# More token columns fetched by SyncE and ScalarE: 102 and 83 in place of 96 and 52

## The chip, the core and the metric

The kernel runs on one core of a Trainium2 chip. The core has five engines that each work through a stream of their own, in order: TensorE (PE, matrix products; PEld is its loading of weights), VectorE (DVE), ScalarE (ACT), GpSimd (POOL) and SyncE (SP, which only issues transfers and waits). They meet through semaphores. ACTq, POOLq and SPq are the issuing side of an engine; ACTq issues transfers and starts ScalarE's activations. Time is device microseconds of one execution; smaller is better.

## What is computed

A recommendation model for 16384 samples: 32 token indices a sample into a table of 50000 x 300 floats, three fields of 20 indices and four of one into small tables of 64 columns, means and concatenation to 748 features, three dense layers with relu, and a sigmoid.

```python
tok = word_emb[token_idx].mean(axis=1)
e1 = emb_mh1[mh1_idx].mean(axis=1)
...
emb = jnp.concatenate([tok, e1, e2, e3, o1, o2, o3, o4], axis=1)
wide = (wide_mh1[mh1_idx].sum(axis=(1, 2)) + ...)[:, None]
h = jax.nn.relu(emb @ W1 + b1)
h = jax.nn.relu(h @ W2 + b2)
h = jax.nn.relu(h @ W3 + b3)
return jax.nn.sigmoid(h @ Wd + bd + wide)
```

## The kernel before

**Tiles and steps.** The samples go in 128 tiles of 128, one sample on each partition. The small tables are not gathered: for each tile the kernel builds one-hot matrices and multiplies them into counts, and the counts times the tables give the sums of the embeddings. That takes 11 steps a tile (STEPS), so the program is a loop of 128 x 11 + 27 = 1435 steps (line 1118). All of it is unrolled: the loop writes the streams of all five engines in one fixed order, and each engine keeps to that order.

**A step.** DVE makes the one-hots of the next step (`hot`, line 776), ScalarE scales half of them in place (line 783), PE multiplies the present step's one-hots into `pc` (line 795), and ScalarE moves the result to `cnt` (line 797). Between these, PE takes a share of the previous tile's table sums (`pg`, line 829) and of the dense layers (`ph`, line 952), whose results ScalarE evicts to `odd` and `even` (line 963).

**Token rows.** A tile has 32 columns of token indices, two to a group, 16 groups. Normally GpSimd fetches a column by one indirect DMA of 128 rows (`gather`, line 258, issued at line 260) into one of six buffers `tok_rows`, and DVE adds the two columns of a group to a sum in PSUM (`own`, `add_up`, line 588), three groups behind the gather in program order (TOK_LAG). A group falls due every 1 / 1.42 steps (`tokens_by`, line 1067).

**Columns that other queues fetch.** Some columns are left out of POOL's list and fetched row by row by SP (column 31 of a tile, buffers `fetched`) or by ScalarE's queue (column 30, buffers `fetched_scalar`), two buffers each. For such a column:

- 4 steps ahead (COLUMN_AHEAD) `load_column` (line 630) issues a DMA on the fetching queue that brings the 128 indices into one row of `columns`;
- 1 step ahead (COLUMN_LAG) `column_offsets` (line 642) has DVE turn them into byte offsets, two operations on `columns`;
- then `fetch` (line 650) loads the offsets into registers, 32 at a time on SP (LOADS) and 16 on ScalarE (SCALAR_LOADS), by the instruction of line 275, and issues one DMA of 1200 bytes for each of the 128 rows (line 244).

`RowFetches` (line 668) sets which tiles have such a column: from a first step on, one column every FETCH_STEPS steps on SP, and every 128 / SCALAR_RATE steps on ScalarE, each given to the next tile whose sum falls due at least three steps after its rows are issued (FETCH_MARGIN). SP's rows are spread evenly over the steps (`Paced_rows`, line 714). ScalarE's are written into a step in two parts: SCALAR_BEFORE rows in front of the scaling of the one-hots, SCALAR_AFTER behind it (lines 1137 to 1142). SP also issues the loads of the index tiles `it` and `ix` (one pair for two tiles) and the stores of the results.

**Program order.** `Program.record` (line 161) works out which earlier instruction of another engine each one must wait for. A wait holds up everything behind it on that engine.

Of the kernel before, what the change touches and what calls it, by code (L numbers as in the profile page):

```python
# [22 lines left out]
N_TOK, TOK_D = 32, 300  # L23
# [5 lines left out]
TOK_BUFS = 6  # L29
HOT_BUFS = 2  # L30
FETCH_FROM = 4
FETCH_STEPS = 14.5
FETCH_MARGIN = 3.0
FETCH_BUFS = 2
COLUMN_AHEAD = 4
# [1 line left out]
LOADS = 32  # L37
LANES = 8
ROW_SEMAPHORES = 8
SCALAR_FROM = 8  # L40
SCALAR_BEFORE, SCALAR_AFTER = 3, 2
SCALAR_RATE = SCALAR_BEFORE + SCALAR_AFTER
SCALAR_MARGIN = 5.0
SCALAR_LOADS = 16
# [332 lines left out]
def kernel(  # L377
# [679 lines left out]
    tiles = B // P  # L1057
# [13 lines left out]
    def summed_at(t):  # L1071

        n = n_groups * (t + 1) + TOK_LAG
        return n / FRONT_PACE if n < front else FRONT_STEPS + (n - front) / pace
# [2 lines left out]

        return summed_at(t) - 1.0

    by_sync = RowFetches(N_TOK - 1, False, summed_at(FETCH_FROM) - FETCH_STEPS - FETCH_MARGIN, FETCH_STEPS, tiles, LOADS)  # L1080
    scalar_steps = P / SCALAR_RATE
    by_scalar = RowFetches(
        N_TOK - 2, True, int(summed_at(SCALAR_FROM) - scalar_steps - SCALAR_MARGIN), scalar_steps, tiles - 2, SCALAR_LOADS
    )
    sync_rows = Paced_rows(by_sync, FETCH_STEPS)

# [162 lines left out]
```

## Time and profile before

| what | us |
|---|---|
| median of 3 runs | 4987.18 |
| lowest and highest | 4986.96, 4992.43 |
| the profiled execution | 4988.4 |
| its span, first to last instruction | 4986.6 |

| engine | busy us | share of the span |
|---|---|---|
| PE | 4794.8 | 96% |
| POOL | 3739.3 | 75% |
| DVE | 3642.8 | 73% |
| ACT | 2728.2 | 55% |

Issuing a DMA, loading a register and waiting on a semaphore don't count as busy, so SP has no row, and ScalarE's busy time leaves out its rows. Lines that a helper records all carry line 113; they are told apart by the tiles that they write and read (`own<-own,tok_rows` is a token sum). In a row of the timeline stand the start, the time from the first to the end of the last of a merged group, engine, line, operation, tiles and count, and in brackets the idle time ahead of it with what ended it. In a row of waits stand who waited for whom, the total, how often, and the longest.

### The profile page before, as it was taken

To read this page: it belongs to the slowest core of one execution; us is meant where nothing else is said; L and a number is where in the kernel's file an instruction comes from. 1 tells how busy PE (TensorE), PEld (TensorE's weight loads), DVE (VectorE), ACT (ScalarE), POOL (GpSimd) and SP (SyncE) were. 2 spreads that over 40 slices of the span, in tenths; PEclk is the share of its full clock that TensorE was granted. 3 is DMA by queue.
4 is the path that set the end of the run, shared out by engine and by line. 5 is a ranking of instruction groups with operands and counts; after the bars stand their busy time and mean duration, and the time that the engine had idled before them with its cause. 6 is when DMAs were issued, how large, how long until landed. Compare 5 with 4: busy or idle time off the path is not lost.

```text
span 4986.6 us, 110478 instructions
## 1 busy us (share of the span) xinstructions
PE 4794.8 (96%) x36356; PEld 3712.3 (74%) x36356; DVE 3642.8 (73%) x6908; ACT 2728.2 (55%) x3658; POOL 3739.3 (75%) x3955
## 2 busy tenths in 40 slices
PE   6699999999999999999999999999999999999999
PEld 4577777777777777777777777767767888888898
DVE  5777777777777777777777777777777777777763
ACT  5455555555555555555555555555555555555552
POOL 7777777777777777777777777777777777777765
PEclk9899999999999999999999999999999999999999
DMA  7444444444444444444444444444444444444443
GB/s 204 127 130 130 130 131 129 131 130 130 131 131 131 130 130 130 131 131 130 130 131 130 131 131 130 130 131 129 131 130 130 130 131 130 131 131 130 131 120 95
DMA packets 305354, 653.28 MB, mean 131 GB/s; under 512 B 157083, under 2 KB 176667, under 8 KB 304775
## 3 DMA queue, kind: packets, MB, share of 16 engines
q0 software_dynamic: 189504, 606.67, 44.7%
q1 hardware_dynamic: 94471, 31.50, 2.9%
q10 hardware_dynamic: 20800, 8.04, 0.8%
q8 instruction: 284, 4.65, 0.4%
q14 instruction: 295, 2.42, 0.2%
HBM read 645.67 MB, written 0.07 MB: 129 GB/s over the span
## 4 chain that ended last, share of the span: by engine, by line
PE 46%; POOL 16%; DMA 15%; DVE 12%; issue 8%; ACT 1%; ACTq 1%; SPq 1%; DVEq 0%; POOLq 0%
PE ph L113 24%; PE pg L113 16%; POOL tok_rows L260 16%; DMA tok_rows<-in_word_emb_dram,it 15%; PE pc L113 6%; DVE own L113 5%; DVE hot L113 4%; DVE g L113 1%; ACTq L244 1%; SPq L244 1%; ACTq L275 0%; ACT cnt L113 0%; DVE x L113 0%; DVE columns L113 0%; ACT hot L113 0%
## 5 line engine op out<-in xcount | busy, mean ns | idle before, releaser
L260 POOL DMA_INDIRECT tok_rows<-in_word_emb_dram,it x3948 | 3738.4, 947 | 1215.6 <-issue 931.5
L113 DVE TENSOR_TENSOR own<-own,tok_rows 128x300 f32<-128x300 f32 x3601 | 1714.5, 476 | 822.0 <-DMA tok_rows<-in_word_emb_dram,it 746.8
L113 ACT ACTIVATE hot<-hot 64x768 bf16<-64x768 bf16 (+1 forms) x1408 | 1155.3, 821 | 1698.2 <-DVE hot L113 1514.8
L113 PE MATMUL pg<-terms,cnt 128*128 128x195 bf16 x17664 | 1721.6, 249 | 31.0 <-DVE g L113 30.7
L113 PEld LDWEIGHTS pg<-terms,cnt 128*128 128x128 fp8e3 x17664 | 1523.8, 98 | 83.7 <-DVE g L113 39.1
L113 PE MATMUL ph<-x,w_sb 128*128 128x384 f32 (+5 forms) x4932 | 1472.1, 436 | 16.5 <-ACT odd L113 11.3
L113 DVE TENSOR_TENSOR hot<-own,sc 128x1656 bf16<-128x1656 bf16 (+1 forms) x1408 | 1386.6, 985 | 86.0 <-PE pc L113 80.4
L113 ACT ACTIVATE cnt<-pc 128x828 uint16<-128x828 f32 (+1 forms) x1408 | 1186.3, 843 | 257.0 <-PE pc L113 170.8
L113 PEld LDWEIGHTS ph<-x,w_sb 128*128 128x128 f32 (+1 forms) x4932 | 829.8, 191 | 306.5 <-ACT odd L113 20.9
L113 PE MATMUL ph<-odd,w_sb 128*128 128x384 f32 (+2 forms) x3328 | 983.2, 434 | 7.7 <-ACT odd L113 7.3
L113 PEld LDWEIGHTS pc<-hot 128*128 128x128 bf16 x8192 | 589.5, 98 | 494.8 <-issue 217.6
L113 PE MATMUL pc<-hot 128*128 128x138 bf16 x8192 | 733.2, 225 | 92.0 <-ACT hot L113 58.7
L113 PEld LDWEIGHTS ph<-odd,w_sb 128*128 128x128 f32 x3328 | 558.7, 191 | 204.7 <-ACT odd L113 15.8
L113 DVE TENSOR_REDUCE g<-pg 128x130 f32<-128x390 f32 (+1 forms) x512 | 259.7, 507 | 216.0 <-PE pg L113 213.1
L113 ACT ACTIVATE odd<-ph,b_sb 128x384 f32<-128x384 f32 (+2 forms) x515 | 270.0, 524 | 134.4 <-PE ph L113 68.8
L113 PE MATMUL ph<-even,w_sb 128*128 128x384 f32 (+2 forms) x832 | 250.0, 436 | 3.3 <-ACT even L113 2.9
L113 PEld LDWEIGHTS ph<-even,w_sb 128*128 128x128 f32 x832 | 142.3, 191 | 56.8 <-ACT even L113 4.1
L113 DVE TENSOR_TENSOR x<-pc,scale 128x768 f32<-128x768 f32 x127 | 120.9, 952 | 74.8 <-PE pc L113 74.0
L113 ACT ACTIVATE even<-ph,b_sb 128x384 f32<-128x384 f32 (+2 forms) x208 | 108.7, 523 | 88.4 <-PE ph L113 65.8
L113 PE MATMUL pc<-ident,g 128*128 128x128 f32 x762 | 106.5, 276 | 11.7 <-ACT cnt L113 7.5
L113 PEld LDWEIGHTS pc<-ident,g 128*128 128x128 f32 x762 | 82.9, 142 | 15.8 <-ACT cnt L113 11.7
L113 DVE COPY sc<-pc 128x512 bf16<-128x512 bf16 x64 | 44.0, 687 | 55.1 <-PE pc L113 55.0
(54 smaller groups left out, 673.0 us busy)
## 6 DMA issues: line engine op xcount, KB each, us to landing
fetched<-in_word_emb_dram SPq DMA_DIRECT2D x12288, 1.2 KB
fetched_scalar<-in_word_emb_dram ACTq DMA_DIRECT2D x6656, 1.2 KB
tok_rows<-in_word_emb_dram,it POOLq DMA_INDIRECT x3948
ix<-in_idx_dram SPq DMA_DIRECT2D x64, 64.0 KB
w_sb<-in_W_dram SPq DMA_DIRECT2D x6, 512.0 KB
it<-in_idx_dram SPq DMA_DIRECT2D x64, 32.0 KB
w_sb<-in_W_dram SPq DMA_DIRECT2D x1, 2048.0 KB
odd<-in_mh_dram SPq DMA_DIRECT2D x3, 682.5 KB
```

The lines of the kernel that those rows point to most:

```text
L113: lambda: call(*args, **operands), self.name, self.name, aps + list(named.values()), outs
L244: return queue.add_instruction(mybir.InstDMACopy(name=self.nc.get_next_instruction_name(), engine=queue.engine, mode="Copy", ins=whole(sou ...
L260: return self.nc.gpsimd.indirect_dma_start(out=out, out_offset=None, in_=table, in_offset=bass.IndirectOffsetOnAxis(ap=index, axis=0),)
```

## The change

Three constants of the two fetch schedules, and the last tile that SP may fetch for.

```diff
-FETCH_STEPS = 14.5
+FETCH_STEPS = 13.5
...
-SCALAR_BEFORE, SCALAR_AFTER = 3, 2
+SCALAR_BEFORE, SCALAR_AFTER = 5, 3
 SCALAR_RATE = SCALAR_BEFORE + SCALAR_AFTER
...
-    by_sync = RowFetches(N_TOK - 1, False, summed_at(FETCH_FROM) - FETCH_STEPS - FETCH_MARGIN, FETCH_STEPS, tiles, LOADS)
+    by_sync = RowFetches(N_TOK - 1, False, summed_at(FETCH_FROM) - FETCH_STEPS - FETCH_MARGIN, FETCH_STEPS, tiles - 1, LOADS)
```

SP gets 13.5 steps for a column in place of 14.5 and fetches 102 columns in place of 96, the first from step 32.16 in place of 31.16, and none of the last tile. ScalarE issues eight rows a step in place of five, five of them in front of the scaling and three behind; a column takes it 16 steps in place of 25.6, and it fetches 83 columns in place of 52, the first from step 72 in place of 63. GpSimd gathers what is left of 4096 columns: 3911 in place of 3948. No other instruction is added or taken away, but the column loads, offsets and register loads that go with the fetched columns.

## The prediction

> **What bounds the kernel now.** The page comes first: its span, its busy shares and the two groups that handle token rows.
>
> ```profile
> span 4986.6 us, 110478 instructions
> ...
> PE 4794.8 (96%) x36356; PEld 3712.3 (74%) x36356; DVE 3642.8 (73%) x6908; ACT 2728.2 (55%) x3658; POOL 3739.3 (75%) x3955
> ...
> PE 46%; POOL 16%; DMA 15%; DVE 12%; issue 8%; ACT 1%; ACTq 1%; SPq 1%; DVEq 0%; POOLq 0%
> ...
> L260 POOL DMA_INDIRECT tok_rows<-in_word_emb_dram,it x3948 | 3738.4, 947 | 1215.6 <-issue 931.5
> ```
>
> PE is busy 96% and GpSimd (POOL) 75%, so PE looks like the bound. The gather row corrects that. A gather has 947 ns of work and 1215.6 / 3948 = 308 ns of idle ahead of it, 1.255 us together, and 3948 x 1.255 = 4954 us: nearly the whole span. So the next question is whether POOL ever waits. POOL's waits and a piece of the middle timeline answer it.
>
> ```profile
> POOL tok_rows L260 <- issue: 931.5, 3054, 0.3
> POOL tok_rows L260 <- DVE own L113: 166.0, 510, 3.3
> POOL tok_rows L260 <- DVE hot L113: 83.9, 275, 0.3
> ```
>
> ```profile
> 2502.87 0.95 POOL L260 DMA_INDIRECT tok_rows<-in_word_emb_dram,it  x1 [0.30 <-issue]
> ...
> 2504.12 0.95 POOL L260 DMA_INDIRECT tok_rows<-in_word_emb_dram,it  x1 [0.30 <-issue]
> ```
>
> The idle ahead of a gather is 0.3 us whether nothing is waited for (931.5 / 3054) or a DVE signal happens to fall into it (166.0 / 510 = 0.33, 83.9 / 275 = 0.31). POOL runs back to back from end to end. DVE stands behind it:
>
> ```profile
> DVE own L113 <- DMA tok_rows<-in_word_emb_dram,it: 769.8, 757, 4.3
> ...
> DVE own L113 <- DMA fetched<-in_word_emb_dram: 11.2, 3, 6.7
> ```
>
> DVE waits 769.8 us for gathered rows, and only 11.2 us for rows that SyncE (SP) fetched. The window view says how much PE has left:
>
> ```profile
> 250.00:4100.00 3850.00, 3766.56 (x27798) 2810.99 (x27798) 2872.23 (x5432) 2129.83 (x2779) 2912.11 (x3076) 1.00 0.49 130
> ```
>
> PE idles 83 us of these 3850. So POOL is the bound, PE stands 2% behind it, and the remaining question is SP. The page has no busy figure for SP, because issuing is not counted. Its timeline has one:
>
> ```profile
> 1999.89 12.64 SPq L244 DMA_DIRECT2D fetched<-in_word_emb_dram  x35
> 2012.58 0.79 SPq L233 DMA_DIRECT2D out_dram<-x  x1
> 2013.42 5.69 SPq L244 DMA_DIRECT2D fetched<-in_word_emb_dram  x18
> 2019.15 0.56 SPq L233 DMA_DIRECT2D columns<-in_idx_dram  x1
> 2019.76 45.20 SPq L244 DMA_DIRECT2D fetched<-in_word_emb_dram  x123
> 2065.00 0.56 SPq L233 DMA_DIRECT2D columns<-in_idx_dram  x1
> 2065.60 7.51 SPq L244 DMA_DIRECT2D fetched<-in_word_emb_dram  x18
> 2073.16 0.41 SPq L233 DMA_DIRECT2D it<-in_idx_dram  x1
> 2073.61 0.71 SPq L233 DMA_DIRECT2D ix<-in_idx_dram  x1
> 2074.37 25.80 SPq L244 DMA_DIRECT2D fetched<-in_word_emb_dram  x71
> ```
>
> SP issues one thing after another with no visible pause. What a column costs it comes from these rows, with the loads of row offsets into registers (line 275), the column loads, and the rows themselves (count, then shortest/median/longest in ns, first and last start in us):
>
> ```profile
> L275 ACTq TENSOR_LOAD <-columns x416: 1178/1294/1532, 255.1 to 4816.2; - x139
> L275 SPq TENSOR_LOAD <-columns x384: 2025/2127/2391, 142.9 to 4905.2; - x192
> L113 DVE TENSOR_SCALAR columns<-columns x296: 203/218/477, 142.4 to 4870.7; 1x128 int32<-1x128 int32 x148
> L233 SPq DMA_DIRECT2D columns<-in_idx_dram x96: 534/554/606, 100.7 to 4852.5; - x96
> ```
>
> ```profile
> L244 SPq DMA_DIRECT2D fetched<-in_word_emb_dram x12288: 211/249/689, 145.0 to 4918.6; - x199
> L244 ACTq DMA_DIRECT2D fetched_scalar<-in_word_emb_dram x6656: 207/263/755, 256.3 to 4825.8; - x196
> ```
>
> The stretch of 123 rows holds four loads of 2.127 us: (45.20 - 8.5) / 123 = 0.298 us a row, its 0.25 us of issue and the gap to the next. A column of 128 rows is 128 x 0.298 + 4 x 2.127 = 46.7 us. Its own column load adds 0.6 (2065.00 to 2065.60). The rest of SP's traffic, start to start: it 0.45 and ix 0.76 us, 64 of each, and out 0.84 us, 52 of them, over 96 columns: 1.3 us. **SP needs about 48.5 us a column.**
>
> What it has comes from the program. Step numbers follow from lines 663 to 685 and 1071 to 1080 by arithmetic: 96 columns start at step 31.16 and every 14.5 steps from there; the last starts at 1408.66, so its column load stands at step 1404 (1408 - COLUMN_AHEAD) and its offsets on DVE at step 1407. First row 145.0, last column load 4852.5: 4707.5 us over 1372.8 steps, **3.43 us a step, 49.7 us for 14.5 steps**. SP is 97 to 98% full already.
>
> **The change part by part.** *Fewer gathers.* 102 and 83 columns replace 96 and 52, so POOL issues 4096 - 185 = 3911 gathers in place of 3948. 37 x 1.255 = 46.4 us leave POOL's stream. The same bytes move on the DMA engines, which are 49% busy (the window row's last but one figure). If POOL stayed the bound, the span would be 4940.
>
> *SP.* 13.5 steps at 3.43 us are 46.3 us, and a column costs 48.5. SP cannot keep that pace; it falls 2.2 us behind with every column. What does this hold up? Column n+1's load is issued by SP itself, 4 steps ahead of that column and so among the rows of column n; DVE turns it into offsets 3 steps later, in DVE's fixed order, in front of the one-hots and every later token sum. So DVE can be at most 3 steps, 10 us, ahead of SP. After some four columns that cushion is used up, and DVE waits at the offsets of each column; behind it stand the sums (then POOL's six buffers fill and POOL waits) and the one-hots (then ScalarE and PE). SP itself waits for nothing by then, since DVE is always early. A step then takes 48.5 / 13.5 = 3.59 us.
>
> The sum: the first column starts one step later, 145.0 + 3.4 = 148.4. The last, 102nd column starts at step 1395.66; its load stands at step 1391, after (1391 - 32.16) / 13.5 = 100.65 columns of SP's work: 100.65 x 48.5 = 4881.5, so at 5030. Landing has no row of its own; it lies between the issue, 0.55, and the 18.2 us from the last load (4852.5) to the last DVE operation on it (4870.7), where nobody was in a hurry. I take 2 us. DVE is then at step 1394. From step 1407 to the end the profiled run took 4986.6 - 4870.7 = 115.9 us, and 13 steps more are 44.6: 160.5. Together **5030 + 2 + 160.5 = 5192.5 us**. Would the last rows come later than that? SP issues them at 148.4 + 102 x 48.5 = 5095; the sum that needs them stands 30 steps behind step 1394, at about 5135. They are in time. Tile 127 is not fetched for any more (tiles - 1), which changes only which tiles are fetched.
>
> The profiled execution took 1.8 us beyond its span (4988.4 beside 4986.6), the median lies 1.2 below it (4987.18). Forecast 5193.
>
> *Bounds of SP's price.* SP's waits view lists 13 sorts of wait between 250 and 4900 us, from
>
> ```profile
> SPq L275 <- DVE own L113: 174.4, 71, 6.8
> ...
> SPq L233 <- DVE columns L113: 0.2, 1, 0.2
> ```
>
> 242 us together. Most are about 2.4 us and end at a load, whose own 2.127 us they contain: a signal that comes during the load counts as awaited. So 242 of 4650 us, 5.2%, is the most that SP can have spare: 49.7 x 0.948 = 47.1 us a column, and 5052 in the sum. On the other side every wait of today stays: 49.7 us a column, 5313. Even the low end is slower, since 102 / 96 asks 6.25% more.
>
> In the Trainium skill, the page "DMA: Bandwidth & Descriptors", section "Latency and other measured facts", gives a register load from memory (tensor_load) a floor of about 600 ns. By that floor a column would be an estimated 4 x 1.53 = 6.1 us cheaper, 42.4, under the 46.3 that it may cost, and POOL's 4940 would hold. The trace disagrees with it as a price: the shortest of 384 loads on SP took 2025 ns, and of 416 on ScalarE 1178.
>
> *ScalarE's queue.* 83 x 128 = 10624 rows in place of 6656, 8 a step in place of 5, and a register load for 16 rows: one in two steps in place of one in 3.2 (664 in all, 416 now).
>
> ```profile
> 2602.25 0.86 ACT L113 ACTIVATE cnt<-pc 128x828 uint16<-128x828 f32 x1 [1.23 <-PE pc L113]
> 2602.27 0.81 ACTq L244 DMA_DIRECT2D fetched_scalar<-in_word_emb_dram  x3
> 2604.80 0.84 ACT L113 ACTIVATE hot<-hot 64x768 bf16<-64x768 bf16 x1 [1.69 <-DVE hot L113]
> 2604.81 0.50 ACTq L244 DMA_DIRECT2D fetched_scalar<-in_word_emb_dram  x2
> ```
>
> Rows go out while an activation runs. Three in front of the scaling took 0.81 us, and the scaling came 1.7 us after them: two more, 0.5 us, fit. In full: 8 x 0.29 + 0.5 x 1.32 = 3.0 us of a step, against 5 x 0.29 + 0.31 x 1.32 = 1.9 now. It fits into 3.59, with 0.6 left for every wait of an in-order queue, where 1.5 are left today. I cost it at nothing because SP's slower step hides it; with that cover gone it could delay the scaling by up to the 1.1 us added. Queued behind a late scaling are the eviction of the counts and the layers' evictions, and PE waits for those.
>
> **The rivals.** *POOL stays the bound: faster.* If SP's column cost at most 46.3 us, all 46.4 us would come out: 4940. PE could follow, with 83 us idle where about 36 are asked for. For it: POOL never rests, and DVE hardly waits for SP's rows today. Against it: the decisive point, 46.3, lies under the 47.1 that the most generous reading of SP's waits gives.
>
> *Both balance.* SP's column at about 46.7, with nothing but rows and register loads: 148.4 + 100.65 x 46.7 + 162.5 = 5011, or nearer 4987 if early cushions carry more. It needs the columns' and index loads to cost nothing, and the timeline shows 0.45 to 0.84 for each.
>
> *ScalarE's stream decides: slower still.* If half of today's 1.5 us of blocked time a step stays, a step takes 3.0 + 0.75 = 3.75 us. From step 72, where its first column starts, to 1400 that is 0.16 x 1328 = 212 over the forecast: 5405. Or its rows lengthen SP's: with SP's rows at ScalarE's 263 ns in place of 249, a column takes 1.8 us more and the sum is 5374. For it: the two queues issue at the same time. Against it: ScalarE's rows hide beside its activations.
>
> The Trainium skill, "Perfetto Trace Analysis", section "DMA Instruction — HWDGE (DVE, Sync)", says that a DMA's profiled time contains a wait for a descriptor generator shared by sequencers. That would be this last mechanism; the 14 ns between the two medians is all that the trace offers for it.
>
> **How the numbers follow.** SP's queue as the bound: 0.80. POOL's 4940: 0.10. Balance: 0.03. ScalarE's stream: 0.07. The likeliest gives 5193. SP's price spans 5052 to 5313; the range goes on to 5375, the lengthened rows, and leaves out the two cases below and ScalarE's worse end. A difference of 0.2%, about 10 us, is what a measurement of this kernel can tell from none. Faster 0.10, same 0.03, slower 0.87.
>
> **What would show it.** Right: SP's rows back to back with 48 to 49 us from one column load to the next; a new wait of DVE at "columns" for SP's column load, some 2 us, a hundred times; POOL's idle ahead of a gather over 0.3 us and its waits for DVE in the hundreds of us; DVE's 769.8 us for gathers mostly gone; PE at about 92% (4794.8 of 5193). Wrong: SP's columns under 46.3 us apart with POOL still at 1.255 us a gather (POOL's case), or DVE waiting for its columns hardly at all while PE waits for "ACT hot" and "ACT cnt" (ScalarE's).

## The result and the profile after

The changed kernel took 5524.05 us (median of 4 runs, 5523.3 to 5525.05) beside 4987.07 (4986.32 to 4992.43) for the kernel before: a ratio of 1.1074, 95% interval 1.1055 to 1.1094. Slower, as forecast, but 330 us over the forecast of 5193 and outside its range. The profiled execution took 5523.77. In six of the runs below (e9 to e11 and e15 to e17) the kernel before took over 7100 us in place of 4990, at a granted clock of 0.88, so their ratios can't be set beside the others.

The page of the changed kernel, its span, its busy shares, the chain and the gathers:

```profile
span 5522.0 us, 115527 instructions
...
PE 4945.6 (90%) x36356; PEld 3776.7 (68%) x36356; DVE 3662.1 (66%) x6982; ACT 2720.4 (49%) x3658; POOL 3702.6 (67%) x3918
...
SPq 36%; PE 24%; DMA 12%; DVE 8%; issue 8%; ACTq 6%; ACT 4%; POOL 2%; DVEq 0%
...
L260 POOL DMA_INDIRECT tok_rows<-in_word_emb_dram,it x3911 | 3701.7, 946 | 1786.9 <-issue 919.5
```

POOL no longer runs back to back: its idle time ahead of the gathers rose from 1215.6 to 1786.9 us, 0.46 us for each. The chain, which went through PE and POOL before, spends 36% in SP's queue and 6% in ScalarE's. PE's own work takes 151 us longer for the same 36356 matmuls (4945.6 against 4794.8); the granted clock of the run is 0.961, before 0.991. The waits view of the changed kernel, who waits for whom, total us, times and the longest:

```profile
POOL tok_rows L260 <- DVE own L113: 741.5, 659, 11.6
...
DVE columns L113 <- DMA columns<-in_idx_dram: 380.6, 76, 11.4
PEld pc L113 <- ACT hot L113: 339.2, 188, 9.4
...
DVE own L113 <- DMA tok_rows<-in_word_emb_dram,it: 221.4, 235, 4.5
...
DVE own L113 <- DMA fetched<-in_word_emb_dram: 151.6, 15, 12.9
...
SPq L244 <- DVE own L113: 73.9, 15, 7.2
```

DVE's wait for gathers fell from 769.8 to 221.4 us; in its place DVE waits 380.6 us for the index columns that SP loads (76 waits of 5 us on the mean, where a hundred of some 2 us were forecast), and POOL 741.5 us for DVE. That is the predicted turn. Not predicted are the two rows with 15 waits each. The tiles `columns` and `fetched` of the changed kernel (count, shortest/median/longest ns, first and last start):

```profile
L275 SPq TENSOR_LOAD <-columns x408: 2027/2129/2374, 144.8 to 5392.4; - x136
L113 DVE TENSOR_SCALAR columns<-columns x370: 204/218/485, 144.3 to 5356.3; 1x128 int32<-1x128 int32 x185
L233 SPq DMA_DIRECT2D columns<-in_idx_dram x102: 532/555/607, 99.8 to 5337.2; - x102
```

```profile
L244 SPq DMA_DIRECT2D fetched<-in_word_emb_dram x13056: 211/252/677, 146.9 to 5403.5; - x198
```

SP's first row starts at 146.9, its last column load at 5337.2, 100.65 columns later: (5337.2 - 146.9) / 100.65 = **51.57 us a column** where 48.5 were forecast. The median of a row moved by only 3 ns (249 to 252), but the mean went from 255.8 to 270.4 (all rows of the trace summed, 3143.8 us / 12288 and 3530.7 / 13056). The timeline between two column loads and the chain in the next stretch show both ends of it:

```profile
2502.40 0.55 SPq L233 DMA_DIRECT2D columns<-in_idx_dram  x1
2502.99 42.43 SPq L244 DMA_DIRECT2D fetched<-in_word_emb_dram  x104
2545.47 0.41 SPq L233 DMA_DIRECT2D it<-in_idx_dram  x1
2545.93 0.61 SPq L233 DMA_DIRECT2D ix<-in_idx_dram  x1
2546.59 6.79 SPq L244 DMA_DIRECT2D fetched<-in_word_emb_dram  x19
2553.49 0.55 SPq L233 DMA_DIRECT2D columns<-in_idx_dram  x1
```

```profile
2605.65 8.58 DMA columns<-in_idx_dram
...
2656.05 9.60 DMA columns<-in_idx_dram
```

104 rows and four register loads take 42.43 us: (42.43 - 8.5) / 104 = 0.326 us a row, where the prediction reckoned with 0.298. And a column load, issued behind those rows, lands 8.6 to 9.6 us after its issue.

**Where the 330 us are.** By the prediction's own terms: the first row came 1.5 us earlier than forecast; SP's column cost 3.07 us more, times 100.65 = 309 us; from the last column load to the last DVE operation on `columns` 5356.3 - 5337.2 = 19.1 us passed in place of 2, 17 us; the rest took 5522.0 - 5356.3 = 165.7 in place of 160.5, 5 us. Nearly all is the price of a column, and of its 309 us the longer issue of the rows is 14.6 ns x 128 x 100.65 = 188. SP's gaps of over 60 ns between two rows grew from 39 us in all to 105, the 15 waits for a buffer (73.9 us) among them.

### The profile page after: what moved, and what is told of

Its sections match the earlier page's. It is cut to its first block, busy times and chain, and to the rows that moved or that the text cites. A ratio compares the mean times of both kernels' runs of the same rounds, so it can differ in the third digit from the quotient of the medians.

```text
span 5522.0 us, 115527 instructions
## 1 busy us (share of the span) xinstructions
PE 4945.6 (90%) x36356; PEld 3776.7 (68%) x36356; DVE 3662.1 (66%) x6982; ACT 2720.4 (49%) x3658; POOL 3702.6 (67%) x3918
## 3 DMA queue, kind: packets, MB, share of 16 engines
q8 instruction: 284, 4.65, 0.3%
## 4 chain that ended last, share of the span: by engine, by line
SPq 36%; PE 24%; DMA 12%; DVE 8%; issue 8%; ACTq 6%; ACT 4%; POOL 2%; DVEq 0%
SPq L244 29%; PE ph L113 12%; PE pg L113 9%; DMA columns<-in_idx_dram 8%; SPq L275 6%; ACTq L244 5%; DVE hot L113 3%; PE pc L113 3%; DVE own L113 3%; DMA tok_rows<-in_word_emb_dram,it 3%; POOL tok_rows L260 2%; ACT hot L113 2%; DMA fetched<-in_word_emb_dram 1%; ACT cnt L113 1%; ACTq L275 1%
## 5 line engine op out<-in xcount | busy, mean ns | idle before, releaser
L260 POOL DMA_INDIRECT tok_rows<-in_word_emb_dram,it x3911 | 3701.7, 946 | 1786.9 <-issue 919.5
L113 PE MATMUL pg<-terms,cnt 128*128 128x195 bf16 x17664 | 1761.8, 252 | 31.1 <-DVE g L113 31.1
L113 PEld LDWEIGHTS pg<-terms,cnt 128*128 128x128 fp8e3 x17664 | 1557.8, 100 | 87.2 <-DVE g L113 35.3
L113 PE MATMUL ph<-x,w_sb 128*128 128x384 f32 (+5 forms) x4932 | 1502.3, 442 | 39.7 <-ACT odd L113 35.3
L113 PEld LDWEIGHTS ph<-x,w_sb 128*128 128x128 f32 (+1 forms) x4932 | 842.9, 194 | 344.1 <-ACT odd L113 54.8
L113 PE MATMUL pc<-hot 128*128 128x138 bf16 x8192 | 748.2, 227 | 352.8 <-ACT hot L113 255.5
L113 PE MATMUL ph<-odd,w_sb 128*128 128x384 f32 (+2 forms) x3328 | 1015.5, 444 | 37.9 <-ACT odd L113 31.9
L113 PEld LDWEIGHTS ph<-odd,w_sb 128*128 128x128 f32 x3328 | 572.3, 195 | 255.0 <-ACT odd L113 50.0
L113 DVE TENSOR_SCALAR columns<-columns 1x128 int32<-1x128 int32 x370 | 89.0, 241 | 389.3 <-DMA columns<-in_idx_dram 380.6
L113 PEld LDWEIGHTS ph<-even,w_sb 128*128 128x128 f32 x832 | 144.6, 194 | 66.9 <-ACT even L113 13.5
L113 DVE TENSOR_TENSOR own<-own,fetched 128x300 f32<-128x300 f32 x102 | 48.1, 472 | 152.5 <-DMA fetched<-in_word_emb_dram 151.6
```

What stands on the lines that cost most here:

```text
L113: lambda: call(*args, **operands), self.name, self.name, aps + list(named.values()), outs
L260: return self.nc.gpsimd.indirect_dma_start(out=out, out_offset=None, in_=table, in_offset=bass.IndirectOffsetOnAxis(ap=index, axis=0),)
```

## The experiments

The diffs are against the changed kernel unless said otherwise, and each ratio is to the kernel before in the same session. For each run the trace's issues and DMA packets were worked into four numbers, used below and put together at the end of this section. Three are of the time between 2000 and 4500 us: the rows a us that SP and ScalarE issue together, the gathers a us, and the share of time in which no DMA packet of any kind was under way on any of the sixteen engines. The fourth, like the mean of a row's issue, is over the whole trace: the backlog, the median time from the end of a row's issue to the start of its packet on SP's queue, the k-th issue against the k-th packet.

### One part at a time

**SP's part alone** (e1_sync_alone).

```diff
-SCALAR_BEFORE, SCALAR_AFTER = 5, 3
+SCALAR_BEFORE, SCALAR_AFTER = 3, 2
```

> SyncE's part of the change alone: 13.5 steps a column, none of the last tile, ScalarE at three rows in front and two behind as before. Theory SP (the prediction's): a row costs SP 0.298 us whatever ScalarE issues, a column 48.5 us, and the time is 5190 to 5290. Theory SHARED: the rows of both queues pass one stage that takes about 4.57 rows/us (17.5 rows a step in 3.82 us with the whole change); here 14.5 rows a step need only 3.17 us of it, so SP's own 3.59 us a step decide: also 5190 to 5290, with rows near 0.256 us mean and no backlog. Theory PLACE (five rows in front of the scaling hold up the step): without them POOL or SP decides, at most 5290. A time near 5520 would refute SHARED and PLACE both and say that SP's column alone costs 51.6 us.

5278.15 us, ratio 1.0572 (1.0541 to 1.0603). Tiles `fetched` and `columns` of this run:

```profile
L244 SPq DMA_DIRECT2D fetched<-in_word_emb_dram x13056: 211/249/763, 147.1 to 5162.7; - x198
```

```profile
L233 SPq DMA_DIRECT2D columns<-in_idx_dram x102: 537/555/1324, 102.8 to 5101.0; - x102
```

(5101.0 - 147.1) / 100.65 = 49.2 us a column, rows at 255.8 ns on the mean, backlog 1.12 us. With ScalarE's rows as before, SP's price is the one forecast within 1.5%.

**ScalarE's part alone** (e2_scalar_alone), the kernel before with ScalarE's new rate:

```diff
-SCALAR_BEFORE, SCALAR_AFTER = 3, 2
+SCALAR_BEFORE, SCALAR_AFTER = 5, 3
```

> ScalarE's part alone: five rows in front and three behind, SyncE at 14.5 steps as before; 3917 gathers. Theory SP: ScalarE's rows cost nobody anything; SP has 49.7 us for a column of 48.5 and POOL decides: 4986 - 31 x 1.255 = 4948. Theory SHARED: 8.8 + 8 = 16.8 rows a step at 4.57 rows/us take 3.68 us in place of 3.43, over the 1330 steps in which both issue: about 5310. Theory PLACE: the step stays at the 3.82 us of the whole change from step 72 on: about 5500.

5329.1 us, ratio 1.0674 (1.0643 to 1.0705). By the prediction this part alone costs SP nothing. The same two tiles:

```profile
L244 SPq DMA_DIRECT2D fetched<-in_word_emb_dram x12288: 211/257/1707, 145.5 to 5254.8; - x199
```

```profile
L233 SPq DMA_DIRECT2D columns<-in_idx_dram x96: 535/554/606, 101.8 to 5188.4; - x96
```

SP issues the same 12288 rows as in the kernel before, 14.5 steps to a column, and its last column load stands at 5188.4 in place of 4852.5. A row takes 283.5 ns on the mean, the backlog is 6.56 us. The chain of this run:

```profile
PE 24%; SPq 24%; ACTq 14%; DMA 13%; DVE 8%; issue 8%; ACT 6%; POOL 3%; DVEq 0%
```

SP's queue, 1% of the chain before, has 24%. **ScalarE's rows alone make SP late.** This run refutes the step that cost them at nothing.

### Not the buffers, not the place, not the bytes of ScalarE's rows, not the loop

**The 15 buffer waits** (e3_no_collision). With 13.5 steps to a column, some columns have their sum so far behind their rows that the first rows of the column after the next are issued into the same of the two buffers before that sum stands in program order (15 times, by the waits above). DVE then waits for those rows, SP's next rows wait for DVE, and by the program order the sum takes those few rows from the later column (the kernel before has this for three columns, its 11.2 us of waits). A shorter margin for SP takes nearer tiles:

```diff
+SYNC_MARGIN = 1.6
...
-                t = next((t for t in tiles_free if wanted_at(t) >= end + FETCH_MARGIN), None)
+                t = next((t for t in tiles_free if wanted_at(t) >= end + (FETCH_MARGIN if by_scalar else SYNC_MARGIN)), None)
```

> The whole change, but SyncE's columns are given to tiles due 1.6 steps or more after their rows in place of 3.0, so that no sum falls due in the step in which the next column but one begins to fill the same buffer. Theory BUFFER: the 15 waits of DVE for fetched rows (151.6 us) and the 15 of SP for DVE (73.9 us) go, and the time falls by 70 to 110, to 5415 to 5455. If these waits only replace others (SP has slack elsewhere), it stays within 20 of 5524.

5491.57 us, ratio 1.0999 (1.0968 to 1.1031). The waits view of this run:

```profile
DVE own L114 <- DMA fetched<-in_word_emb_dram: 48.6, 9, 13.7
...
DVE columns L114 <- DMA columns<-in_idx_dram: 441.7, 88, 13.6
```

SP's 15 waits of 73.9 us fall to 3 of 9.3, but only 32 us come out, less than expected; a row still takes 272.4 ns and the backlog is 5.13 us. DVE's waits for `columns` grew meanwhile (380.6 to 441.7). The collisions explain about a tenth of the miss.

**The place of ScalarE's rows** (e6_three_in_front): 3 in front of the scaling and 5 behind.

```diff
-SCALAR_BEFORE, SCALAR_AFTER = 5, 3
+SCALAR_BEFORE, SCALAR_AFTER = 3, 5
```

> The whole change with three of ScalarE's eight rows in front of the scaling and five behind. Theory PLACE (the five in front hold up the scaling, and that sets the step): the time falls by more than 50. Theory SHARED (the two queues' rows pass one stage at about 4.57 rows/us): it stays within 25 of 5524, since as many rows are issued.

5528.36 us, ratio 1.1083 (1.1061 to 1.1105): the same. Where in the step they stand doesn't matter here.

**The bytes of ScalarE's rows** (e4_short_scalar_rows): 64 in place of 1200.

```diff
+        size = ROW_BYTES if name == "SP" else SHORT_BYTES
+        out = out[:, 0:size]
...
-            source = table[:, bass.ds(value(), ROW_BYTES)]
+            source = table[:, bass.ds(value(), size)]
```

> The whole change, but each of ScalarE's row transfers brings 64 bytes in place of 1200; the sums leave out the rest of those rows. ScalarE issues as many instructions in the same places. Theory SHARED by data (what the two queues share is the moving of bytes): SP's column goes back from 51.6 to 48.5 to 49.5 us, the backlog of 4.9 us from issue to packet to about 1, and the time to 5200 to 5320. Theory SHARED by issue (a price for each transfer, whatever its size): 5480 to 5530. Theory PLACE: 5480 to 5530 as well, without a change of SP's rows.

5529.62 us, ratio 1.1076 (1.1044 to 1.1108): the same again. It is not the bytes of ScalarE's rows.

**The loop through the column load** (e11_columns_early, e13_columns_early_again): SP's column load stands among its own late rows, so a late row could make itself later. Eight steps ahead in place of four open that loop.

```diff
-COLUMN_AHEAD = 4
+COLUMN_AHEAD = 8
```

> The whole change with the column loads issued 8 steps ahead in place of 4. Theory SHARED: DVE's 380 us of waits for columns move to other places (fetched rows, buffers), since the queues' rows set the pace: within 25 of 5524. Theory LOOP (the column loads land 9 us after their issue, behind the rows, and SP and DVE wait for each other over them): the time falls by 60 or more.

The first run took 7245.28 us beside 7127.05 for the kernel before. There rows go at 3.53 a us, and the ratio of 1.017 (1.0141 to 1.02) says nothing of a limit at 4.57. Again, where the kernel before took 4994.71:

> The same kernel as e11_columns_early, column loads 8 steps ahead, since e11 ran where the kernel before took 7127 us with a granted clock of 0.88, and tells nothing. Theory SHARED: within 25 of 5524. Theory LOOP (SP and DVE wait for each other over column loads that land 9 us late): 60 or more below.

5529.74 us, ratio 1.1069 (1.1037 to 1.1102). The waits of DVE for `columns` fall from 380.6 us to 71.2 and stand elsewhere in the same view:

```profile
DVE own L113 <- DMA fetched<-in_word_emb_dram: 426.4, 37, 22.6
...
DVE columns L113 <- DMA columns<-in_idx_dram: 71.2, 19, 8.6
```

So the column load is where lateness showed, not where it arose.

### The rows as packets

**Four pieces to a row** (e5_split_rows): the row is described as 4 pieces of 300 bytes, to see whether several packets a row lighten or load the queue.

```diff
-            source = table[:, bass.ds(value(), ROW_BYTES)]
+            source = table[:, bass.ds(value(), ROW_BYTES)].rearrange("p (a b) -> p a b", a=PIECES)
...
-                    outs=whole(out),
+                    outs=whole(out.rearrange("p (a b) -> p a b", a=PIECES)),
```

> The whole change, with each row transfer described as four pieces of 300 bytes in place of one of 1200, on both queues. The number of transfers and their places stay. Theory ENGINE: the shared stage is one DMA engine that carries every row of both queues, one packet of each queue in turn with the gathers' 4800-byte packets; four pieces go to several engines, the backlog between a row's issue and its packet falls from 4.9 us to about 1, and the time goes to that of SP's own price, 5200 to 5300. Theory FRONT: the shared stage lies ahead of the DMA engines and has a price for each transfer; then the time stays at 5480 to 5530, or rises with four pieces.

5525.51 us, ratio 1.1078 (1.1055 to 1.11). The packets were 1200 bytes still: the contiguous pieces were joined, so the run is the changed kernel once more.

**Four pieces kept apart** (e10_pieces_apart): each piece goes to a place 304 bytes from the last, and the sum reads them from there.

```diff
+PIECES, PITCH = 4, 76
...
-    fp = Ring(pool, [P, TOK_D], F32, "fetched", FETCH_BUFS)
+    fp = Ring(pool, [P, PIECES * PITCH], F32, "fetched", FETCH_BUFS)
```

> The whole change with each row written as four pieces of 300 bytes that lie 304 bytes apart in the buffer, so that they cannot be joined into one packet (the packets of the run before this show that its four pieces were joined to 1200 bytes, so it tried nothing). Theory ENGINE (one DMA engine carries all rows): pieces go to four engines, the backlog and the longer rows go, 5200 to 5300. Theory FRONT with a price for each transfer: 5480 to 5530. Theory FRONT with a price for each packet: four times the packets, far slower, 6500 and more.

11071.04 us beside 7127.05, ratio 1.5541 (1.5496 to 1.5586). Tile `fetched`:

```profile
L245 SPq DMA_DIRECT2D fetched<-in_word_emb_dram x13056: 3/618/2179, 197.5 to 10936.6; - x198
```

A row of four packets takes SP 0.615 us of issue on the mean, without a backlog (0.98 us). The packets cost time at the issue, 0.12 us for each beyond the first. At half the rows a us the run can't show a limit on one-packet rows, but its packets are used below.

### GpSimd's gathers

**Short gathers** (e8_short_gathers): 240 bytes of each gathered row in place of 1200.

```diff
-                out=out,
+                out=out[:, 0:SHORT],
...
-                in_=table,
+                in_=table.rearrange("n (a d) -> (n a) d", d=SHORT),
```

> The whole change, but each gather brings 60 floats a row in place of 300, from other places of the table; the rest of those rows is left out of the sums. Theory ENGINE: the rows wait in turn with the gathers' packets, which now are short; the backlog falls to about 1 us and the time to 5200 to 5300. Theory FRONT: the gathers' bytes do not matter, 5480 to 5530.

5434.67 us, ratio 1.0895 (1.0874 to 1.0917); backlog 6.01 us. Four fifths of the gathers' bytes are worth 90 us, of 296 that come out with no gathers at all (the next runs).

**No gathers** (e9_no_gathers, e14_no_gathers_again) and **half of them** (e12_half_gathers):

```diff
-                    program.gather(f"gather{tokp.slot}", rows[-1], word, it[:, j : j + 1], batch, tok_rows)
```

> The whole change without GpSimd's gathers: the sums take zeros for those columns, SP's and ScalarE's rows stay as they are. Theory QUEUES (the stage that takes 4.57 rows/us is met by the two queues alone): the steps stay at 3.82 us, the backlog at about 5 us, and the time at 5450 to 5530. Theory THREE (the gathers take part of the same stage): the backlog falls to about 1 us, SP's column to 48.5 to 49.5, and the time to 5200 to 5300, SP's own price.

5229.11 us, where the kernel before took 7127.05 (ratio 0.734, 0.7319 to 0.7362). Again, where it took 4994.71:

> The same kernel as e9_no_gathers, where the kernel before takes about 4990 us. Theory THREE (the gathers share the stage of the rows): as in e9, backlog under 1 us, SP's column 48.5 to 49.5 us, 5200 to 5300. If e9 was fast because of the chip that it ran on, the backlog is 3 us or more and the time 5450 to 5530.

5227.96 us, ratio 1.0465 (1.0435 to 1.0496), the same time in both. Tile `fetched`, and its rows together with those of `fetched_scalar`, from 2000 to 4500 us:

```profile
L244 SPq DMA_DIRECT2D fetched<-in_word_emb_dram x13056: 211/249/559, 125.1 to 5118.2; - x198
...
L244 SPq DMA_DIRECT2D fetched<-in_word_emb_dram x6537: 211/251/559, 2000.0 to 4499.9; - x199
```

```profile
L244 ACTq DMA_DIRECT2D fetched_scalar<-in_word_emb_dram x5516: 207/265/619, 2000.1 to 4499.8; - x197
```

(6537 + 5516) / 2500 = 4.82 rows a us, with a backlog of 0.62 us and rows of 254.4 ns. All the rows of the changed kernel go out at SP's own price if nobody gathers. The same window of the changed kernel:

```profile
L244 SPq DMA_DIRECT2D fetched<-in_word_emb_dram x6210: 211/252/674, 2000.0 to 4499.0; - x195
```

```profile
L244 ACTq DMA_DIRECT2D fetched_scalar<-in_word_emb_dram x5229: 207/266/632, 1999.9 to 4499.8; - x194
```

(6210 + 5229) / 2500 = 4.58. Half the gathers, with their full length:

```diff
-                    program.gather(f"gather{tokp.slot}", rows[-1], word, it[:, j : j + 1], batch, tok_rows)
+                    if r:
+                        program.gather(f"gather{tokp.slot}", rows[-1], word, it[:, j : j + 1], batch, tok_rows)
```

> The whole change with only the second gather of each group; the first column of each group is left out of the sums and read as zeros. Without any gather the backlog was 0.63 us and 4.82 rows/us went through; with all of them 4.9 us and 4.57. Theory COUNT (each gather takes the rows' stage for a time of its own, whatever its bytes: with a fifth of the bytes 4.65 rows/us was reached): half as many gathers leave the two queues below the cap, backlog 1 us or little more, time 5210 to 5320. Theory ANY (gathers under way at all, however few, halve the turns of the rows): backlog 3 us or more and 5400 to 5530.

5262.77 us, ratio 1.0535 (1.0504 to 1.0566). Its two tiles in the same window:

```profile
L244 SPq DMA_DIRECT2D fetched<-in_word_emb_dram x6501: 211/249/628, 1999.9 to 4499.6; - x197
```

```profile
L244 ACTq DMA_DIRECT2D fetched_scalar<-in_word_emb_dram x5475: 207/265/737, 1999.9 to 4499.8; - x196
```

(6501 + 5475) / 2500 = 4.79 rows a us, backlog 0.87 us, rows of 256.7 ns. Half the gathers are enough to free the rows, though four fifths of their bytes were not.

**All gathers, half their rows** (e15_half_rows, e16_half_rows_again, e17_half_rows_third):

```diff
-                out=out,
+                out=out[0:HALF],
...
-                in_offset=bass.IndirectOffsetOnAxis(ap=index, axis=0),
+                in_offset=bass.IndirectOffsetOnAxis(ap=index[0:HALF], axis=0),
```

> Every gather of GpSimd fetches only the first 64 of its 128 rows, the other 64 rows of its buffers stay zero; the 3911 gathers are all still issued, and SP's and ScalarE's rows are those of the changed kernel. In the traces so far the packets of the fetched rows, of both queues, hardly ever overlap in time (0.5% of it in the changed kernel, though one is under way in 42%), while the 16 shares of a gather do: so the rows seem to pass one of the sixteen DMA engines, which has its sixteenth of every gather to carry too. That engine is nearly never free where the rows were late (no packet of any kind under way in 0.1 to 1.8% of the time between 2000 and 4500 us), and was free more often elsewhere (9.2% before the change, 25% with half the gathers, 47% with none). What is open is what a gather costs that engine: not its bytes (gathers of 240 bytes a row left 5434.67 us). Theory ELEMENTS: it is the rows of the gather, eight for each engine, four here. Then this run goes like the one with half the gathers: 5230 to 5300 us, 4.75 rows a us or more, a median backlog of a row below 1.5 us, no packet under way in 10 to 40% of the time. Theory GATHERS: each gather takes a fixed turn whatever is in it. Then it goes like the one with short rows: 5400 to 5500 us, at most 4.66 rows a us, a backlog of 4 to 6 us, no packet in under 3%.

7305.37 us where the kernel before took 7138.6, ratio 1.0237 (1.0198 to 1.0276).

> The kernel of e15_half_rows once more: there the kernel before took 7138.6 us, at a granted clock of 0.88, so that the rows were asked for at a lower rate and nothing of the question could be seen. Where the kernel before takes about 4990 us, the numbers expected are the same. ELEMENTS: 5230 to 5300 us, 4.75 rows a us or more, a median backlog below 1.5 us, no packet under way in 10 to 40% of the time. GATHERS: 5400 to 5500 us, at most 4.66 rows a us, a backlog of 4 to 6 us, no packet in under 3%.

7367.79 beside 7217.72, 1.0203 (1.0178 to 1.0229).

> The kernel of e15_half_rows a third time, since the kernel before took over 7100 us on both runs so far and the rows were asked for too slowly there. At the same rates there (3.5 rows and 0.54 gathers a us) no packet was under way in 40.6% of the time with half-length gathers and in 27.5% with whole ones (e11_columns_early), which leans to ELEMENTS. Where the kernel before takes about 4990 us, the numbers expected are the same. ELEMENTS: 5230 to 5300 us, 4.75 rows a us or more, a median backlog below 1.5 us, no packet under way in 10 to 40% of the time. GATHERS: 5400 to 5500 us, at most 4.66 rows a us, a backlog of 4 to 6 us, no packet in under 3%.

7287.07 beside 7133.39, 1.0212 (1.0172 to 1.0251). In all three the rows go at 3.5 a us, below the limit, so none can show the choice that it was made for. At the same 3.5 rows and 0.54 gathers a us no packet was under way in 40.6% of the time with half the rows in a gather (e15_half_rows) and in 27.5% with all (e11_columns_early). But half the rows are half the bytes too, and this share counts all sixteen engines, so it doesn't tell a cost for each gathered row from one for each gather.

### A smaller step

**Six rows a step** (e7_six_rows): the kernel before with one more row behind the scaling, 62 columns for ScalarE and 3938 gathers.

```diff
-SCALAR_BEFORE, SCALAR_AFTER = 3, 2
+SCALAR_BEFORE, SCALAR_AFTER = 3, 3
```

> The kernel before with six rows a step on ScalarE, three and three, and SyncE as before: 62 and 96 columns, 3938 gathers. Theory SHARED: 8.8 + 6 = 14.8 rows a step need 3.25 us at 4.57 rows/us, under the 3.43 of a step, so POOL stays the bound and ten gathers go: 4987 - 12.5 = 4974. If queueing below the cap already lengthens SP's rows by 1.2 us a column or more, SP's reserve is gone and the time is 4990 to 5060.

4981.89 us (10 runs) beside 4988.24 (13 runs), ratio 0.9989 (0.9979 to 0.9998): ahead of the kernel before by some 6 us, a tenth of a per cent and half of what was expected. Rows at 255.9 ns, backlog 1.22 us. ScalarE can take a fifth more; what it can't take is what came with eight.

### The runs side by side

| run | rows a us | gathers a us | backlog us | no packet | row of SP, mean ns |
|---|---|---|---|---|---|
| e1_sync_alone | 3.98 | 0.75 | 1.12 | 12.9% | 255.8 |
| before | 4.04 | 0.80 | 1.14 | 9.2% | 255.8 |
| e7_six_rows | 4.33 | 0.80 | 1.22 | 6.3% | 255.9 |
| after | 4.58 | 0.71 | 4.92 | 1.0% | 270.4 |
| e2_scalar_alone | 4.58 | 0.74 | 6.56 | 0.1% | 283.5 |
| e3_no_collision | 4.59 | 0.71 | 5.13 | 0.5% | 272.4 |
| e4_short_scalar_rows | 4.57 | 0.71 | 5.49 | 1.1% | 269.6 |
| e6_three_in_front | 4.58 | 0.71 | 5.00 | 0.9% | 269.9 |
| e13_columns_early_again | 4.57 | 0.71 | 5.40 | 1.6% | 273.9 |
| e8_short_gathers | 4.65 | 0.72 | 6.01 | 1.8% | 260.4 |
| e12_half_gathers | 4.79 | 0.37 | 0.87 | 25.2% | 256.7 |
| e14_no_gathers_again | 4.82 | 0 | 0.62 | 47.1% | 254.4 |

Two groups: where no packet is under way in 6% of the time or more, the median row goes out within 1.2 us of its issue; where that share is under 2%, the backlog is four to five times that, and the rate stands at 4.57 to 4.59 rows a us (4.65 with short gathers), whatever was edited.

The packets say which stage that is. In the changed kernel the packet of some fetched row is under way in 42% of this window, but two of them at once in only 0.5%: the rows of both queues pass one after the other. In e10_pieces_apart, where a row is four packets, two or more are under way in 4.1% of the window, of 19.8% in which any is: pieces kept apart do run side by side. The 32 packets of 4800 bytes of a gather run about 16 at a time. With no row under way exactly one gather packet is under way in 19% of the window (8% before the change): a part of a gather that is still to be done when the others are through.

Such gather packets fit exactly between the rows. Between the packets of the two queues lie 3151 gaps of over 150 ns, 53% of the window, and 2860 of them begin and end, to within 15 ns, with one gather packet or with two in a row. If the gaps are moved by 0.1 to 5 us, only 214 to 249 still do. So **the rows of both queues go through one of the sixteen DMA engines, in turn with that engine's share of every gather.** The gaps that no gather packet fills in this way are 5% of the window in the changed kernel and 42% in the kernel before: the engine had room, and is now nearly always taken. The packet records don't name their engine, so that it is one is inferred from this fit.

In the Trainium skill, page "DMA: Bandwidth & Descriptors", section "Why a DMA increments its semaphore by 16 and not by 1", the number of engines of a DMA follows from the slowest dimension of its access pattern that is not 1, a one-element transfer takes one engine, and DMAs of SP's and ScalarE's queues take the lowest-numbered ones. The page does not say it for a single run of 1200 bytes, which is what a row is; if such a run counts as one, the rows of both queues share one engine, and the trace agrees, with two row packets at once in 0.5% of the time. No run here shows which engine it is.

What runs out there is not simply the time of the packets. With 64-byte rows on ScalarE's queue (e4_short_scalar_rows) a row's packet is under way in 24% of the window in place of 42, but the gather packets found in the gaps last 497 ns on the mean in place of 382. With short gathers (e8_short_gathers, 16 packets of 1920 bytes each) the packet of a row of SP takes 175 ns at the median in place of 53. What one side gives up, the other's packets take longer; why, no run here shows.

## Why the prediction was right or wrong

**Right: SP's queue becomes the bound.** The chain has it at 36%, DVE waits 380.6 us at `columns`, POOL waits for DVE, the waits for gathers are mostly gone and PE stands at 90% (forecast 92%). The rivals with POOL as the bound or a balance are out. In the whole change, though, the pace of SP's queue is set by the stage behind it.

**Right within 1.5%: SP's own price of a column.** 49.2 us with SP's part alone and 49.0 without gathers ((5052.8 - 125.1) / 100.65, from the last row below), forecast 48.5. Tile `columns` of e14_no_gathers_again:

```profile
L233 SPq DMA_DIRECT2D columns<-in_idx_dram x102: 533/556/651, 87.9 to 5052.8; - x102
```

**Wrong, and the step that failed: "I cost it at nothing because SP's slower step hides it"**, said of ScalarE's added rows. With SP's part alone the time was 5278.15, 85 us over the forecast; ScalarE's part added the other 246. The step looked only at whether ScalarE's own queue has time for its rows. But 60 rows in a hundred more on that queue also pass the engine that SP's rows pass, and SP's column went from 49.2 us to 51.57; in e2_scalar_alone they make SP late with its own rows unchanged. With 4.58 rows a us, the measured rate, as the limit the whole time follows: ScalarE's first column load stands at 275.9 and its first rows near 290, when SP has issued some 370 of its rows; the other 13056 + 10624 - 370 = 23310 take 23310 / 4.58 = 5090 us, so the last row goes out at about 5380. It went at 5403.5, and 5522.0 is 118.5 us behind it.

**Named, but sized wrongly: "its rows lengthen SP's".** That rival had the right two queues and the wrong size, 5374, and too low a chance. It took the 14 ns between two medians as the effect; the medians hardly move (249 to 252), while the mean moves by 14.6 to 27.7 ns and the waits between rows come on top. Beside it stood the Trainium skill's wait for a descriptor generator shared by sequencers ("Perfetto Trace Analysis", section "DMA Instruction — HWDGE (DVE, Sync)"). SP's rows don't show it with the two queues at 4.82 rows a us and no gathers (e14_no_gathers_again: 254.4 ns a row, 255.8 before the change); the gathers have to be there.

**Wrong: the landing of a column load at 2 us.** It took 8.6 to 9.6 us, since it queues behind the same late rows. In SP's steady pace this costs once, 17 us at the end.

**Missed: the two buffers.** With a column every 13.5 steps and some sums more than a column later, SP meets its buffer's last user 15 times, against "SP itself waits for nothing by then". About 32 us, by e3_no_collision.

**The range** went up to the lengthened rows at a price read in the kernel before; with SP's price bounded by "every wait of today stays" it assumed that the price of an issue does not depend on how many rows others issue. That is the assumption that fell.

What stays open: what a gather costs the shared engine, whether by its rows or by its count, and why its packets and the rows' stretch each other; that the bytes are the smaller part is shown (90 of 296 us).

## What to carry to other kernels

A price for an issue that is read at one load holds for that load: before adding DMAs to a second queue, set the packets of all queues against each other, and see whether some of them never overlap and how long the stage that they share is free. A queue with no busy figure can be a bound at 97%, and a second one can fill the stage behind it without being full itself. When a producer's pace is shortened, compare the distance between a buffer's uses with how late its reader may be.

## What the hardware showed unexpectedly

- One-row DMAs of two queues, 1200 bytes each, passed at 4.57 to 4.59 a us together beside 0.71 to 0.74 gathers a us, and 64-byte rows on one of the queues changed nothing (4.57); without gathers 4.82 went through with nothing late.
- A row's packet takes 53 ns at the median, 72 on the mean before the change and 92 after it, when it alternates with a gather's packets.
- A row of four packets took 0.615 us to issue (e10_pieces_apart), a row of one 0.256; pieces that lie next to each other went as one packet of 1200 bytes (e5_split_rows).
- In the changed kernel, where PE waits more, its 36356 matmuls take 4945.6 us in place of 4794.8, at a granted clock of 0.961 in place of 0.991.
- In e11_columns_early, at a granted clock of 0.884, PE pauses over 1 us between matmuls with nothing awaited that the profile shows. Its chain between 3000 and 3003 us:

```profile
3000.88 0.24 PE pg L113
3001.12 1.15 issue
3002.27 0.24 PE pg L113
3002.52 1.16 issue
```

e9_no_gathers, on the same chip in the same session, ran at a clock of 0.976 and took 5229.11 us, so the gathers have a part in it. What makes PE pause, no run here tells.
